# Turning the a2 terms of the attention layer on VectorE before they are stored to DRAM, and storing them from ScalarE's queue

## The chip, the cores and the metric

The kernel runs on one core of one Trainium2 chip. The metric is device time in microseconds (us) of one execution of the program; shown are the median of several executions and, beside it, one execution that was profiled. The engines are TensorE (PE, with its weight loads as PEld), VectorE (DVE), ScalarE (ACT), GpSimd (POOL) and SyncE (SP). SP, ACT and POOL also issue DMA transfers, each from its own queue; SPq, ACTq and POOLq in the profile are those queues.

## The reference, cut to what matters

Two layers work on N = 4096 nodes with C = 512 features, float32, with a dense 4096 x 4096 adjacency `adj`. Layer 0 averages the first 64 neighbours of each node, applies two linear maps with leaky ReLU, adds the input and normalizes the rows. Layer 1 is graph attention over its result `x`:

```python
Wh    = h @ W + bW
Wha1  = Wh @ a1 + b1          # one number per node
Wha2  = Wh @ a2 + b2          # one number per node: "the a2 terms"
e     = Wha1[:, None] + Wha2[None, :]
e     = where(e > 0, e, 0.2 * e)
e     = where(adj > 0, e, -9e15)
h_new = softmax(e, axis=1) @ Wh
x     = layernorm(x + h_new)
```

The change concerns only how the 4096 numbers of `Wha2`, computed with a node per partition, are laid out as a row that every partition can read.

## The kernel before, in words

Nodes are kept in 32 blocks of 128. Blocks 2t and 2t+1 hold the even and odd rows of the same 256 nodes, so node number = 256 t + 2 p + r for partition p and r = 0 or 1. The order of instructions on each engine is written out by hand; a tile framework only adds the waits. Each transfer that SP or ACT issues takes one of eight completion semaphores, which the program reuses in turn: an issue waits until the earlier transfer on the same semaphore has landed. SP and ACT share these eight. POOL's transfers have eight of their own.

Layer 0 runs first. Its second half is 2048 large matmuls on PE (L750), 128 for each pair of blocks of the adjacency, and `finish(i, g)` closes one block at a time: it makes the new row block, stores it to DRAM as `x1_d` (L719, POOL), and forms the products with the folded attention vectors, which leave Wha2 and Wha1 of block i in columns 0 and 1 of `e12` (`e12` is 128 partitions x 4 x 32 blocks; L724).

Layer 1 begins with a transition, and this is where the change lies. In DVE's order: the end of `finish` for block 31; small operations of 128x32 on the counts (L1132 to L1135); the addition of the biases to `e12` columns 0 and 1 (L1138, two instructions). In ACT's order: one logarithm of 128x32 into `e12` column 2 (L1136). Then POOL issues four kinds of transfer:

- `e12` column 0, stored to `e2_d` in DRAM (L1139, shown as `e_d<-e`): 16 KB. `e2_d` is indexed [t, p, r], so a partition p contributes, for each t, the two numbers r = 0 and 1. Source and target have only these two numbers, 8 bytes, in a run.
- `e12` columns 1 to 3, stored to `st_d` (L1142), 384 bytes a partition.
- `e2_d` read back as four quarters, each broadcast to 32 partitions, into `e2_n` (L1145, `e_n<-e_d`): 4 x 128 KB.
- `st_d` read back into `st_n` (L1147): 4 x 48 KB.

Meanwhile PE computes Wh = x W in steps j = 0 to 31 of 128 rows. Each step needs a turned block of x. `load_turned(j)` on SP (L807, shown as `w<-x_d`, as its tile is part of a tile named w) reads it in four transfers of 64 KB, in pieces of 512 bytes, into one of four slots (j mod 4); `turn_x1(j)` on DVE (L833) turns it in 32x32 squares into its operand form and frees the slot. Steps 0 to 3 are plain (matmuls L1185, ACT copies the result out of PSUM at L1189). The later steps, in pairs g = 2 to 15, use a scheme with seven products (`seven_wh`, matmuls L887). In it DVE forms sums of the turned blocks (L876, L877 at once, L882, L883 a step later), ACT copies a partial product (L906), and DVE adds it (L915, L911 for the first pair) into the PSUM bank into which PE then accumulates. `combine_wh` (L846 to L849) is DVE's work on finished pairs. The order on DVE around pair 3 is: `turn_x1(8)`, L882, L883, L846 to L849, `turn_x1(9)`, L876, L877, L915.

ACT issues the first loads of the adjacency codes, `load_nat` (L940, `nat<-code_d`, eight transfers of 64 KB), four after the first two copies L1189 and four after the third. Their first use is `cover` (L952, ACT), followed by `mask` on DVE (L962), which reads `e2_n`, and `score` (L945), which reads `st_n`. These weights of the attention fill a tile called `early`, until then scratch space; its quarter 3 is unused in its first 512 columns.

After step 31 PE runs the attention products (L1067) without a pause to the end.

Of the kernel before, what the change touches and what calls it, by code (L numbers as in the profile page):

```python
# [21 lines left out]
SQ = 32  # L22
# [10 lines left out]
def two_layer_adj_gnn(  # L33
# [16 lines left out]
    nc = tc.nc  # L50
# [3 lines left out]
    NT = NB // 2  # L54
# [35 lines left out]
    e12 = const.tile([P, 4, NB], F32, name="e12")  # L90
# [3 lines left out]
    e2_d = dram.tile([NT, P, 2], F32, name="e2_d")  # L94
# [42 lines left out]
    with ExitStack() as l0:  # L137
# [145 lines left out]
        with ExitStack() as la:  # L283
# [47 lines left out]
            def early(name):  # L331
                dt = I32 if name == "a" else BF16
                t = adj_p.tile([P, CH], dt, name=name).bitcast(F32)
                return t.rearrange("p (c q) -> p c q", q=C)

            raw = {}
            for name in ("nb", "line"):
                t = early("a")
                raw[name] = [t[:, c, :] for c in range(NC)]
            raw["w"] = []  # L340
            for k in range(2):
                t = early("left")
                raw["w"] += [t[:, c, :] for c in range(NC // 2)]
            early_rows = []
            for k in range(2):
                t = early("edge")
# [252 lines left out]
            for g in range(1, EDGE // 2):  # L599
                steps = idle  # L600
                q = done[0]
# [129 lines left out]
        for s in range(NB * NS):  # L731
            i, g = divmod(s, NS)
# [46 lines left out]
    early = wp.tile([P, NI, NS * SQ], F32, name="w")  # L779
# [356 lines left out]
    nc.scalar.activation(e12[:, 2, :], cnt, AF.Ln)  # L1136
    for k in range(2):
        nc.vector.tensor_scalar_add(e12[:, 1 - k, :], e12[:, 1 - k, :], ca[:, k : k + 1])  # L1138
    nc.gpsimd.dma_start(  # L1139
        e2_d.rearrange("t p r -> p t r"), e12[:, 0, :].rearrange("p (t r) -> p t r", r=2)  # L1140
    )
    nc.gpsimd.dma_start(st_d, e12[:, 1:4, :])  # L1142
    for n in range(4):
        quarter = e2_d.rearrange("(n t) p r -> n (t p r)", n=4)[n]
# [104 lines left out]
    p, rz = banks[NT - 1], rzs[NT - 1]  # L1249
# [62 lines left out]
```

## Time and profile before

| | us |
|---|---|
| median of 3 executions | 1566.76 (1563.01 to 1566.88) |
| the profiled execution | 1566.57 |
| its span | 1564.8 |
| PE busy in the span | 1549.1 (99%) |
| DVE, ACT, POOL busy | 1261.9, 980.1, 268.7 |
| first L1185 matmul, first L887 matmul, first L1067 matmul, from the span's start | 678.42, 692.15, 785.01 |

The span is the time from the first to the last instruction that the profiler recorded; 1.77 us of the execution lie outside it. Every time below that is a point in the execution counts from the span's start. In a row of the profile "out<-in" names the tiles written and read, and "[4.89 <-DVE acc L915]" says how long the engine idled before it and what ended that idleness. A row of the stretch view gives, for a stretch of time, the busy time of each engine with its number of instructions, then the clock that TensorE was granted as a share of its full one (PEclk), the mean busy share of the 16 DMA engines, and the bytes that they moved per second.

### The profile page before, as it was taken

How to read it: one execution, taken by the hardware profiler on the slowest of the kernel's cores; microseconds unless marked ns; L12 is line 12 of the kernel's file. 1: busy time of each engine (PE TensorE's matmuls, PEld its weight loads, DVE VectorE, ACT ScalarE, POOL GpSimd, SP SyncE). 2: the span in 40 equal slices, each digit the busy share in tenths (PEclk: the TensorE clock that was granted, in tenths of full speed). 3: DMA queues.
4: the chain of work that ended last, by engine and by line, in shares of the span. 5: the costliest groups of instructions: out<-in, count | busy, mean ns of one | idle time of the engine just before them, and what ended most of it. 6: DMA issues, size and time to landing. Idle time of an engine off the chain costs nothing.

```text
span 1564.8 us, 19133 instructions
## 1 busy us (share of the span) xinstructions
PE 1549.1 (99%) x6587; PEld 1244.3 (80%) x6587; DVE 1261.9 (81%) x2337; ACT 980.1 (63%) x1183; POOL 268.7 (17%) x425
## 2 busy tenths in 40 slices
PE   9999999999999999999999999999999999999998
PEld 5444468888888888868888888888888888888887
DVE  6888658999999998458888888787878878888765
ACT  2676558888888878426784675555765557755530
POOL 4454212222222122120001001110011100111101
PEclk9999999999999999999999999999999999999999
DMA  8866468999898787653222122221222212222102
GB/s 235 204 218 202 156 181 252 256 237 273 243 260 254 231 241 221 140 120 103 63 55 53 36 61 69 54 68 24 59 69 54 68 35 48 68 56 66 44 11 54
DMA packets 175345, 201.17 MB, mean 129 GB/s; under 512 B 101920, under 2 KB 135488, under 8 KB 167056
## 3 DMA queue, kind: packets, MB, share of 16 engines
q1 hardware_dynamic: 147472, 130.33, 29.8%
q0 software_dynamic: 26272, 67.66, 16.9%
q10 hardware_dynamic: 1504, 1.97, 0.5%
q8 instruction: 51, 0.84, 0.2%
q14 instruction: 46, 0.38, 0.1%
HBM read 141.03 MB, written 42.08 MB: 117 GB/s over the span
## 4 chain that ended last, share of the span: by engine, by line
PE 95%; DMA 2%; DVE 1%; issue 1%; ACT 0%; SPq 0%; POOLq 0%; ACTq 0%; DVEq 0%
PE acc L1067 35%; PE acc L750 30%; PE pt L1067 14%; PE acc L498 7%; PE acc L887 5%; PE acc L372 3%; DMA a<-in_adj_dram 1%; DMA nat<-code_d 1%; PE acc L1185 0%; PE pt L372 0%; PE pt L153 0%; DMA w<-x_d 0%; DVE edge L389 0%; DMA xb<-in_x_dram 0%; ACT edge L175 0%
## 5 line engine op out<-in xcount | busy, mean ns | idle before, releaser
L1067 PE MATMUL acc<-bt,s 128*128 128x256 f32 x1504 | 335.7, 379 | 0.0
L750 PE MATMUL acc<-y_hi,kt 128*128 128x512 f32 x824 | 320.5, 389 | 0.0
L750 PE MATMUL acc<-y_lo,kt 128*128 128x512 f32 x824 | 320.5, 389 | 0.0
L1067 PEld LDWEIGHTS acc<-bt,s 128*128 128x128 f32 x1504 | 285.8, 190 | 38.9
L952 ACT ACTIVATE w<-nat,few 128x1024 f32<-128x1024 uint8 x128 | 137.0, 1137 | 237.7 <-DVE a L1027 237.7
L1067 PE MATMUL acc<-bt,a 128*128 128x256 f32 x1056 | 239.0, 379 | 0.0
L1067 PE MATMUL pt<-bt,a 128*128 128x256 f32 x992 | 224.5, 379 | 0.0
L1067 PEld LDWEIGHTS acc<-bt,a 128*128 128x128 f32 x1056 | 200.6, 190 | 27.3
L1067 PEld LDWEIGHTS pt<-bt,a 128*128 128x128 f32 x992 | 188.5, 190 | 25.6
L277 ACT ACTIVATE kt<-ktb,few 128x1024 fp32r<-128x1024 uint8 x124 | 142.8, 1151 | 96.8 <-PE acc L750 79.6
L1027 DVE STREAM_TRANSPOSE a<-w 128x1024 f32<-128x1024 f32 x128 | 153.1, 1226 | 61.8 <-ACT w L1008 51.0
L126 POOL TENSOR_TENSOR rs<-ve,few 128x1 f32<-128x1 f32 x64 | 46.5, 726 | 809.7 <-DVE ve L124 797.1
L750 PEld LDWEIGHTS acc<-y_lo,kt 128*128 128x128 f32 x824 | 154.7, 188 | 32.2
L750 PEld LDWEIGHTS acc<-y_hi,kt 128*128 128x128 f32 x824 | 154.6, 188 | 32.1
L945 ACT ACTIVATE w<-w,st_n 128x1024 f32<-128x1024 f32 x128 | 149.3, 1233 | 16.1 <-DVE m L962 16.1
L1008 ACT ACTIVATE w<-w,nm 128x1024 f32<-128x1024 f32 x128 | 145.5, 1138 | 11.1 <-DVE nm L999 11.1
L962 DVE CUSTOM_DVE_ANT_0 w<-e_n,w 128x1024 f32<-128x1024 f32 x128 | 149.5, 1222 | 1.3
L175 ACT ACTIVATE edge<-a,few 128x2048 bf16<-128x2048 int32 x64 | 136.2, 2128 | 8.6 <-DMA a<-in_adj_dram 4.5
L223 ACT CAST code<-left 128x2048 uint8<-128x2048 bf16 x64 | 121.1, 1893 | 0.0
L206 DVE TENSOR_TENSOR left<-edge,left 128x2048 bf16<-128x2048 bf16 x64 | 78.4, 1225 | 2.2
L298 POOL DMA_DIRECT2D c<-in_x_dram x120 | 65.8, 555 | 69.7 <-DVE xt L325 54.3
L194 DVE TENSOR_TENSOR_SCAN left<-few,ends,left 128x1024 bf16<-128x1024 f32 x32 | 75.2, 2352 | 1.1
(225 smaller groups left out, 2009.6 us busy)
## 6 DMA issues: line engine op xcount, KB each, us to landing
a<-in_adj_dram SPq DMA_DIRECT2D x64, 1024.0 KB, 6.1
code_d<-code POOLq DMA_DIRECT2D x64, 256.0 KB, 4.3
nat<-code_d SPq DMA_DIRECT2D x248, 64.0 KB, 2.2
w<-x_d SPq DMA_DIRECT2D x128, 64.0 KB, 2.2
own<-in_x_dram SPq DMA_DIRECT2D x31, 256.0 KB, 3.2
own<-own_d POOLq DMA_DIRECT2D x31, 256.0 KB, 5.0
x_d<-own POOLq DMA_DIRECT2D x31, 256.0 KB, 5.0
c<-in_x_dram POOLq DMA_DIRECT2D x120, 64.0 KB, 5.0
```

Of the source, the lines that this page charges most:

```text
L175: nc.scalar.activation(edge_of[s], loaded.pop(s).rearrange("p (t q) -> p q t", q=2), AF.Sigmoid, bias=steep[:, 0:1], scale=STEEP, accum_ou ...
L206: nc.vector.tensor_tensor(left, e, left, ALU.mult)
L223: nc.scalar.copy(code.bitcast(U8).rearrange("p (t q) -> p q t", q=2), seen_of.pop(s))
L277: nc.scalar.activation(kts[s], bytes_.rearrange("p t (i r) -> p t r i", r=2), AF.Sigmoid, bias=steep[:, 1:2], scale=STEEP,)
L498: nc.tensor.matmul(bank, lhs[:, k, :], rhs[:, k, :], start=start and k == 0, stop=k == 1, skip_group_check=True,)
L750: nc.tensor.matmul(accs[i], kt[:, k // 2, k % 2, :], term[j], start=(j == 0 and term is y_hi), stop=(j == NB - 1 and term is y_lo),)
L945: nc.scalar.activation(dst, src, AF.Prelu, bias=bias, scale=scale, alpha=0.2)
L952: nc.scalar.activation(wts[b][:, i, :], nats[b, i // 2].bitcast(U8)[:, i % 2, :], AF.Relu, bias=far, scale=-FAR,)
L962: nc.vector.tensor_tensor_reduce(w_i, e2_n, w_i, 1.0, -3e38, ALU.subtract, ALU.max, m4s[b][:, i : i + 1])
L1008: nc.scalar.activation(w_i, w_i, AF.Exp, bias=nms[b][:, i : i + 1], accum_out=z4s[g][:, r, i : i + 1])
L1027: nc.vector.transpose(a[:, r].rearrange("p s (i a) -> p i s a", a=SQ), wts[2 * g + r][:, :, ts(k, 8 * SQ)].rearrange("p i (s x) -> p i s x ...
L1067: nc.tensor.matmul(banks[g][n], lhs[:, j, :], bt[:, 4 * k + j, rhs, :], start=(k == 0 and j == 0 and n == mate[0]), stop=(k == NP - 1 and ...
```

## The change

The a2 terms are turned in DVE's 32x32 squares before they are stored. Two transposes (r = 0 and 1), each of 128x32, write into 64 unused columns of the tile `early`. In each group of 32 partitions the 32 columns read are the 16 values of t of column 0 of `e12` and, as a filler, the 16 of column 1. After them partition 32 q + t holds the numbers of nodes 256 t + 64 q up to 64 q + 63 in a run of 64 numbers, 256 bytes. Four transfers (one for each q), each of 16 partitions, store them. They are issued from ACT's queue, after the logarithm L1136 and ahead of the first copy L1189 (L1194 in the changed file), whereas the store before was issued by POOL. Contents and layout of `e2_d` are the same. Lines below the change move down by five.

```diff
-    nc.gpsimd.dma_start(
-        e2_d.rearrange("t p r -> p t r"), e12[:, 0, :].rearrange("p (t r) -> p t r", r=2)
-    )
+
+    e2_t = early[:, 3, : 2 * SQ]
+    for r in range(2):
+        nc.vector.transpose(e2_t[:, r::2], e12[:, 0:2, r::2])
+    for q in range(4):
+        nc.scalar.dma_start(
+            e2_d.rearrange("t (q i) r -> q t (i r)", q=4)[q], e2_t[SQ * q : SQ * q + NT, :]
+        )
     nc.gpsimd.dma_start(st_d, e12[:, 1:4, :])
```

## The prediction

> **What bounds the kernel now.** I read the page first, then the chain of waits around the transition, then stretches of time, then DMA issues. The page says that PE is nearly always busy and carries the chain:
>
> ```profile
> PE   9999999999999999999999999999999999999998
> ...
> PE 95%; DMA 2%; DVE 1%; issue 1%; ACT 0%; SPq 0%; POOLq 0%; ACTq 0%; DVEq 0%
> ```
>
> So little is to be had: only time in which PE stands still or runs slowly. The chain, asked for from 670 to 800 us, shows the one place where the middle of the kernel leaves PE:
>
> ```profile
> 685.86 0.04 issue
> 685.90 0.44 ACTq L940
> ...
> 686.86 9.66 DMA nat<-code_d x2
> ...
> 697.41 1.26 SPq L807
> 698.67 0.05 issue
> 698.72 4.55 DMA w<-x_d
> ...
> 703.74 0.72 DVE a L833
> ...
> 705.29 0.43 DVE acc L915
> 705.72 0.04 issue
> 705.76 79.41 PE acc L887 x356
> ```
>
> Read backwards: PE resumed at 705.76 when L915 ended, L915 stood behind turn_x1(9), this waited for load_turned(9), and its issue waited for a nat transfer. The order of instructions in the timeline gives the idleness, and the stretch view gives the clock and the DMA:
>
> ```profile
> 705.76 2.07 PE L887 MATMUL acc<-s,bt 128*128 128x256 f32 x4 [4.49 <-DVE acc L915]
> ```
>
> ```profile
> 688.00:690.00 2.00, 2.00 (x6) 0.81 (x5) 1.86 (x3) 0.59 (x1) 0.39 (x1) 1.00 0.99 146
> 690.00:692.00 2.00, 2.00 (x6) 0.95 (x5) 1.33 (x3) 0.00 (x0) 0.00 (x0) 1.00 0.88 53
> 692.00:694.00 2.00, 2.00 (x9) 1.33 (x7) 0.88 (x3) 0.59 (x1) 0.00 (x0) 1.00 0.85 29
> ...
> 702.00:704.00 2.00, 0.00 (x0) 0.00 (x0) 0.26 (x1) 0.00 (x0) 0.00 (x0) 0.82 1.17 213
> 704.00:706.00 2.00, 0.24 (x1) 0.24 (x2) 1.93 (x5) 0.00 (x0) 0.00 (x0) 0.50 0.59 130
> 706.00:708.00 2.00, 2.00 (x5) 1.61 (x6) 1.90 (x6) 0.13 (x1) 0.00 (x0) 0.50 0.52 136
> 708.00:712.00 4.00, 4.00 (x15) 3.32 (x14) 2.15 (x5) 1.64 (x3) 0.00 (x0) 0.74 0.43 121
> ```
>
> Two things stand there. PE stops from 701.27 to 705.76, and its clock is halved from about 703.3 to 710.1 (0.82 of the first stretch, 0.74 of the last). And from 690 to 694 the DMA engines are 85% busy while moving 29 to 53 GB/s, against 146 and 213 around it. What is in flight then is e_d<-e, issued at 686.66 and landed 9.1 us later, and everything beside it is slow: from 690 to 694 the issues answer
>
> ```profile
> nat<-code_d ACTq DMA_DIRECT2D x2, 64.0 KB, 7.6
> w<-x_d SPq DMA_DIRECT2D x1, 64.0 KB, 7.1
> ```
>
> where the page's medians for these transfers from SP's queue are 2.2 us. I conclude that the 4096 pieces of 8 bytes clog the DMA engines until 695, and that the nat transfer issued at 688.92 therefore lands at 696.5; load_turned(9) uses its semaphore next, so it is issued from 696.58, not 691, and lands at 703.3.
>
> **What the Trainium skill says.** "DMA: Bandwidth & Descriptors", Specifications, asks for 512 bytes or more per piece and says that smaller ones are read, modified and written; its Rules for kernel authors say that a strided last dimension gives a descriptor per element. The trace fits the slowness (29 GB/s) but shows no read of the target. The same page, Issuing engines are not separate DMA queues, says that transfers of all queues share the 16 engines: nat (ACT) and w (SP) slowed by a POOL store agree. "TensorE: Matmul & The Clock Gate", What's actually happening, has the clock halve after about 3.4 us idle and return after as long busy: the trace has a stop of 4.49 us, and half clock for some 6.8 us.
>
> **The change, part by part.**
>
> *Removed: the clog.* L915 for pair 3 then no longer waits for a load. What is late next is DVE itself: it was ready for turn_x1(8) at 696.44 but started at 698.34 (idle 1.90, released by DMA w<-x_d). From that start to the end of L849 took 698.34 to 701.41, 3.07 us; from the start of turn_x1(9) to the end of L915, 703.74 to 705.71, 1.97 us. So 696.44 + 3.07 + 0.1 + 1.97 = 701.58, and PE resumes at 701.62, after an idleness of 0.35. Gain on the stop: 705.76 - 701.62 = 4.14 us.
>
> *Removed: the half clock.* 20 matmuls ran from 705.76 to 712.31, 6.55 us; at full clock a matmul of L887 starts every 0.216 us (28 in 6.04 us from 714.04), so 4.32. Gain 2.23. A stop of 0.9 us at 694.04 shows no drop, so none is expected after 0.35.
>
> *Does the load come in time?* turn_x1(9) is due at 699.6. load_turned(7) goes out once turn_x1(3) is done, at 686.6, and SP's issues follow each other 0.43 to 0.48 us apart in the trace. In the changed program every issue of loads 8 and 9 reuses the semaphore of an issue about four places ahead, so SP has four transfers of 64 KB under way, and a load of four takes about as long as one transfer takes to land. With 2.2 us each, load 8 goes out from 689.3 and load 9 from 691.9 to 693.7, landing by 696; with 3.5 us each, from 692.9 to 695.0, landing by 698.5. But e_n and st_n (0.7 MB) now run from about 690, not from 697, beside them; in their company loads took 4.1 to 5.2 us before. Both were then queued at once; here the start is spread. I take 3.5 and keep 5 as the bad end.
>
> *Added: two transposes on DVE.* Not in the trace at this size. From below, a 128x32 operation takes 0.18; from above, the 128x512 transpose L833 0.71. I take 0.2 each, 0.4 in all; nothing excludes 1.4, and in an in-order queue a gain is excluded. Behind them are turn_x1(3) to (5). PE wants turn_x1(3) for step 3 at 688.7 and has it at 686.5 instead of 686.05. DVE then idles 0.74 before L1196 and 1.57 before L911, both for PE or ACT following PE, so 0.4 is absorbed: 0.
>
> *Added: four issues on ACT's queue.* L940 issues show 0.43 to 0.48 apart: 4 x 0.45 = 1.8 us, from 685.95 (after the transposes) to 687.7. Behind them: copies L1189 0 and 1 move from 685.5 to some 687.9 and 688.4, the first four nat from 685.5-687.3 to 688-689.8, copy 2 from 688.9 to about 689.8, the other nat to 690.3-692.2, copy 3 to 692.4 against 692.35. ACT idled 2.37 and 2.85 us before copies 2 and 3, which is the cover. PE wants the bank of copy 2 at 692.15, and L906 at 694.07 follows copy 3, so copy 3 (0.59 us) may start at 693.4. I take 0; with transfers at 3.5 us the semaphore reuse moves copy 3 to about 694.2 and costs 0.7. A gain from this is excluded. The nat data is wanted at 708.14, over 10 us later.
>
> *The landing of the stores.* Nearest rows: z_d<-z, 4 KB, 1.4 us; x_d<-w, 256 KB, 2.3 us. I take 1.4 to 2.3. SP's load 7 reuses semaphores of the second and third store: its third issue moves from 687.45 to 688.4 at most, in the schedule above already.
>
> *Moved off POOL.* Its issue of 1.18 us goes; st_d may go at once; e_n waits for four ACT stores, from about 689.5 and not 696.27. First use of e_n is L962 at 712.39, so this gains nothing itself.
>
> **Sum.** 4.14 + 2.23 = 6.4 us gained, 0 to 0.7 lost: 6.2. After 706 PE waits nowhere for more than 0.3 us, and shifting PE, DVE and ACT together keeps that: from pair 6 on the L915s wait for PE again (idle 0.86, 1.77). Pair 5 is the narrow one: L915 comes 6.74 + 4.6 us after that of pair 3, its use two periods of 6.04 later, slack some 0.4. So profiled time 1566.57 - 6.2 = 1560.4, and against the median, 0.2 above that execution, 1560.5.
>
> **Rivals.**
>
> *A. The transfers collide instead* (22%). e_n, st_n, nat and loads 7 to 9 all run from 688 to 697. At 5 us each, load 9 is issued from 694.4 and lands at 701, L915 ends at 703 and PE stops 1.8 us: 2.7 gained, with the clock 4.9. For it: DMA share over 1 from 698 to 704. Against it: by packet times these transfers fill only some 6 of 10 us. Time 1561.9 to 1564.1.
>
> *B. Slower: ACT's queue is held* (6%). The pieces are still under 512 bytes. If the first store took 9.1 us as e_d did, the nat transfer that reuses its semaphore, and with it copies 2 and 3 and L906, wait: nat at 695, copy 3 at 699.5, L906 at 700.3 against 694.07. PE loses 6.2 where it lost nothing, with half clock 2.2, while the old 6.7 is only partly there: +2, 1569. It decides from a landing of 3.3 us on, when copy 3 passes 693.4. Against it: 64 pieces where 4096 were, and z_d<-z lands in 1.4.
>
> *C. The clog is not the pieces* (6%): the change doesn't do what it says, the slow transfers are congestion by count. Then time stays at 1566 to 1567. Against it: in no other stretch between 684 and 720 do the engines move so little at such a share (at 1.17 they move 213 GB/s).
>
> **Numbers.** The main case has 66%, at 1559.5 to 1561.5 before noise. A measurement of this kernel can tell about 0.3%, 4.7 us, from no change; the executions before spread 3.9 us. Main case and the upper part of A are faster: 0.73; the rest of A, C and a share of noise 0.22; B 0.05. The range takes the main case with the spread down, and A and most of C up: 1557 to 1565.5.
>
> **What would show it.** Right: no stretch of low GB/s at 85% share after 688; w and nat landing under 4 us; PE idle under 1 us between 694 and 712; PEclk 1.00 throughout; first L1067 matmul near 778.8, not 785.0; two 128x32 transposes of some 0.2. Wrong: a new stop of PE at 692 behind L1194 or L906 (B), load 9 landing after 699.6 (A), e_d landing over 3.3 us.

## The result, and the profile after

| | before | after |
|---|---|---|
| median of 8 executions, us | 1566.24 (1563.01 to 1566.88) | 1560.98 (1560.69 to 1564.03) |
| profiled execution, its span, us | 1566.57, 1564.8 | 1561.81, 1559.9 |
| PE busy in the span, us | 1549.1 | 1546.9 |
| first L1067 matmul, us from the span's start | 785.01 | 778.81 |

The ratio after/before is 0.9973, with a 95% interval of 0.9962 to 0.9984, which is 4.2 us of 1566. The medians lie 5.3 apart because six of the eight executions before took 1566.2 to 1566.9 and two 1563.0 and 1563.7, and the median lies in the upper group. The forecast was 1560.5.

On the page, PE's busy slices are what they were, and so, within one per cent, are the shares of the chain. A change of a third of a per cent is not seen there:

```profile
PE   9999999999999999999999999999999999999998
...
PE 95%; DMA 2%; DVE 2%; issue 1%; ACT 0%; ACTq 0%; POOL 0%; POOLq 0%; DVEq 0%
```

It is seen in the chain of waits from 670 to 800 us (columns: start, us, what). The link "nat transfer of 9.66 us, then a late load" is gone. The nat transfer takes 2.00. But the chain still runs through the loads of turned blocks, 8 and then 9, before it comes back to PE at 701.71, not 705.76:

```profile
685.49 0.35 ACTq L1144
...
687.63 2.00 DMA nat<-code_d
689.63 0.03 issue
689.65 5.25 DMA w<-x_d
694.92 4.64 DMA w<-x_d
...
699.68 0.72 DVE a L833
...
701.23 0.43 DVE acc L915
701.66 0.04 issue
701.71 77.27 PE acc L887 x356
```

In the timeline, PE's stop ahead of L915 fell from 4.49 to 0.76, and DVE shows why 0.76 is left: `turn_x1(9)` waited 0.59 for its load.

```profile
701.71 1.13 PE L887 MATMUL acc<-s,bt 128*128 128x256 f32 x4 [0.76 <-DVE acc L915]
```

```profile
699.68 0.71 DVE L833 STREAM_TRANSPOSE a<-w 128x512 f32<-128x512 f32 x1 [0.59 <-DMA w<-x_d]
```

The stretches (PE, PEld, DVE, ACT, POOL, then PEclk, DMA share and GB/s) show the two effects that the forecast named. From 690 to 694 the DMA engines, about as busy as before, now move 187 to 252 GB/s and not 29 to 53. From 702 on the clock is 1.00:

```profile
690.00:692.00 2.00, 2.00 (x6) 0.94 (x5) 1.66 (x4) 0.03 (x1) 2.00 (x5) 1.00 0.96 187
692.00:694.00 2.00, 1.71 (x8) 1.15 (x7) 0.55 (x2) 0.84 (x2) 1.62 (x3) 1.00 0.81 252
...
702.00:704.00 2.00, 2.00 (x11) 1.74 (x11) 1.90 (x6) 1.13 (x2) 0.00 (x0) 1.00 0.54 134
704.00:706.00 2.00, 2.00 (x11) 1.77 (x10) 1.93 (x5) 0.67 (x2) 0.00 (x0) 1.00 0.53 137
```

Of the DMA issues, the store (`e_d<-w`) and `st_d`, issued from 684 to 690, land in 1.7 and 1.8 us. Before, they took 9.1 and 8.4 (first the kernel before, issues from 683 to 689.5, then the changed kernel):

```profile
st_d<-e POOLq DMA_DIRECT2D x1, 48.0 KB, 8.4
e_d<-e POOLq DMA_DIRECT2D x1, 16.0 KB, 9.1
```

```profile
e_d<-w ACTq DMA_DIRECT2D x4, 4.0 KB, 1.7
st_d<-e POOLq DMA_DIRECT2D x1, 48.0 KB, 1.8
```

But those issued from 690 to 694 still take over 5 us, in company now of `e_n` and `st_n`, which have moved up to 689.4 and later:

```profile
nat<-code_d ACTq DMA_DIRECT2D x4, 64.0 KB, 5.3
w<-x_d SPq DMA_DIRECT2D x4, 64.0 KB, 5.5
```

One slip in the forecast: the store before had 2048 pieces of 8 bytes (16 KB), not 4096. No step of its sum used the number.

### The profile page after: what moved, and what is told of

Same layout as the page of the kernel before. It is cut to its first block, busy times and chain, and to the rows that moved or that the text cites. A ratio compares the mean times of both kernels' runs of the same rounds, so it can differ in the third digit from the quotient of the medians.

```text
span 1559.9 us, 19141 instructions
## 1 busy us (share of the span) xinstructions
PE 1546.9 (99%) x6587; PEld 1242.7 (80%) x6587; DVE 1261.9 (81%) x2339; ACT 980.1 (63%) x1183; POOL 266.4 (17%) x424
## 4 chain that ended last, share of the span: by engine, by line
PE 95%; DMA 2%; DVE 2%; issue 1%; ACT 0%; ACTq 0%; POOL 0%; POOLq 0%; DVEq 0%
PE acc L1067 35%; PE acc L750 30%; PE pt L1067 14%; PE acc L498 7%; PE acc L887 5%; PE acc L372 3%; DMA a<-in_adj_dram 1%; DMA w<-x_d 1%; PE pt L372 0%; PE pt L153 0%; PE acc L357 0%; DVE edge L389 0%; ACT edge L175 0%; DMA nat<-code_d 0%; DVE y_lo L421 0%
## 5 line engine op out<-in xcount | busy, mean ns | idle before, releaser
L1067 PE MATMUL acc<-bt,s 128*128 128x256 f32 x1504 | 335.7, 379 | 0.0
L1067 PEld LDWEIGHTS acc<-bt,s 128*128 128x128 f32 x1504 | 285.8, 190 | 38.9
L1067 PE MATMUL acc<-bt,a 128*128 128x256 f32 x1056 | 239.0, 379 | 0.0
L1067 PE MATMUL pt<-bt,a 128*128 128x256 f32 x992 | 224.5, 379 | 0.0
L1067 PEld LDWEIGHTS acc<-bt,a 128*128 128x128 f32 x1056 | 200.6, 190 | 27.3
L1067 PEld LDWEIGHTS pt<-bt,a 128*128 128x128 f32 x992 | 188.5, 190 | 25.6
```

The costliest lines, as they stand in the source:

```text
L1067: nc.tensor.matmul(banks[g][n], lhs[:, j, :], bt[:, 4 * k + j, rhs, :], start=(k == 0 and j == 0 and n == mate[0]), stop=(k == NP - 1 and ...
```

## The experiments

Two theories of why the time fell. **P**: the 8-byte pieces clog the DMA engines for everybody, and their going is the gain. **Q**: the gain comes from the move to ACT's queue, or from what moved with it. Ratios are to the kernel before, measured in the same session. Medians of the kernel before ranged from 1563.5 to 1566.2 between sessions, so ratios are compared, not medians.

### The changed kernel again, and its stores back on POOL's queue

The first is the changed kernel once more, for a ratio in the same session. The second differs from it in one thing:

```diff
-        nc.scalar.dma_start(
+        nc.gpsimd.dma_start(
             e2_d.rearrange("t (q i) r -> q t (i r)", q=4)[q], e2_t[SQ * q : SQ * q + NT, :]
```

> The changed kernel once more, beside the others on the same chip. Both theories: 5 to 6 us under the kernel before, PE stop ahead of L915 of pair 3 under 1 us, no half clock between 690 and 1550.

> The turned a2 terms (pieces of 256 bytes), but their four stores issued by POOL. Theory P (the 2048 pieces of 8 bytes clog the DMA engines): no stretch of low GB/s, loads land in under 5.5 us, within 1.5 us of the changed kernel, so 4 to 6 us under the kernel before. Theory Q (it is the queue: the store generated in software on POOL, or its late issue, is what costs): no gain, within 1.5 us of the kernel before, PE stop near 4.5 us.

Measured: 0.9974 [0.9964, 0.9984] for the changed kernel, 4.2 us between the medians and not the 5 to 6 expected, and 0.9971 [0.9960, 0.9981] with POOL's queue. On POOL the stretches move 207 to 247 GB/s, and PE does not stop at L915 at all:

```profile
688.00:690.00 2.00, 2.00 (x6) 0.89 (x5) 1.53 (x4) 0.00 (x0) 1.19 (x3) 1.00 0.72 207
690.00:692.00 2.00, 2.00 (x10) 1.39 (x8) 1.03 (x3) 0.58 (x1) 2.00 (x5) 1.00 1.02 237
```

The queue is worth nothing that these runs resolve (about 1.5 us); the new layout alone gives the gain.

### The 8-byte store on ACT's queue

The kernel before, with its store issued by ACT. This is the other half of the change:

```diff
-    nc.gpsimd.dma_start(
+    nc.scalar.dma_start(
         e2_d.rearrange("t p r -> p t r"), e12[:, 0, :].rearrange("p (t r) -> p t r", r=2)
```

> The kernel before, with its one store of 8-byte pieces issued by ACT where the changed kernel issues its four; no transposes. Theory P: the clog comes 1 us earlier and stays some 6 us long, transfers in it land in 7 us or more, PE stops for 3 us or more and the clock halves; time within 2 us of the kernel before, or slower, if ACT's queue is held behind it. Theory Q: 4 to 6 us under the kernel before.

Measured: 1.0007 [0.9999, 1.0015], no gain. The store lands in 7.9 us, and the clog is there, earlier, from 684:

```profile
686.00:688.00 2.00, 2.00 (x6) 0.95 (x5) 1.59 (x3) 0.59 (x1) 0.00 (x0) 1.00 0.59 19
688.00:690.00 2.00, 2.00 (x6) 0.87 (x5) 1.60 (x4) 0.00 (x0) 0.00 (x0) 1.00 0.74 36
```

PE now stops twice (the profiled execution is the slowest of thirteen, 2.7 us over their median):

```profile
695.38 1.13 PE L887 MATMUL acc<-s,bt 128*128 128x256 f32 x4 [3.61 <-DVE acc L911]
704.71 2.07 PE L887 MATMUL acc<-s,bt 128*128 128x256 f32 x4 [3.02 <-DVE acc L915]
```

The first stop is rival B's mechanism: ACT's nat issues wait for slow transfers, the copy and L906 stand behind them, and DVE's L911 waits 4.2 us for L906. Rival B's mechanism is thus a real danger of a slow store on ACT's queue; in the changed kernel the stores land in 1.7 us and it does not arise. Of the two halves of the change the layout carries the gain, and Q falls.

### The half clock by itself

The kernel before with its clog, but PE fed with ten matmuls of no use ahead of the one that waits for L915 (one spare PSUM bank, nothing reads it):

```diff
+            if g == PLAIN + 1:
+                idle = ps_s.tile([P, 2, HC], F32, name="pt")
+                for _ in range(10):
+                    nc.tensor.matmul(
+                        idle[:, 0], w11[:, 0, :P], w11[:, 0, :], start=True, stop=True,
+                        skip_group_check=True,
+                    )
             if new:
                 product_wh(xv[:, 0], sum_x(g, 2), t2)
```

> The kernel before, with ten matmuls of 128x256 (20 records, 4.3 us at full clock) of no use put on PE where it stops ahead of L915 of pair 3, into an idle PSUM bank. The clog and the wait stay. If the stop costs a half clock of 2.23 us beside its own 4.49, the clock stays at 1.00, PE resumes at the same 705.8, and the time is 1.8 to 2.4 us under the kernel before. If the half clock costs nothing (what follows is bound by DVE or ACT anyway), the time stays within 0.7 us of the kernel before.

Measured: 0.9988 [0.9982, 0.9995], which is 1.9 us of some 1564 (0.8 to 2.8). The clog stays, the useless work fills the stop, and the clock does not drop:

```profile
690.00:692.00 2.00, 2.00 (x9) 1.33 (x7) 0.91 (x3) 0.58 (x1) 0.00 (x0) 1.00 0.56 25
...
704.00:706.00 2.00, 2.00 (x11) 1.77 (x10) 1.93 (x6) 1.42 (x2) 0.00 (x0) 1.00 0.51 146
```

So some 2 us of the gain are the half clock, as the forecast's step of 2.23 had it, and the rest is the stop.

### Pieces of 32 bytes

The changed kernel, whose transposes leave gaps, so that the four stores have 512 pieces of 32 bytes, not 64 of 256:

```diff
-    e2_t = early[:, 3, : 2 * SQ]
+    e2_t = early[:, 3, : 4 * SQ].rearrange("p (a z) -> p a z", z=16)
...
-        nc.vector.transpose(e2_t[:, r::2], e12[:, 0:2, r::2])
+        nc.vector.transpose(e2_t[:, :, r:8:2], e12[:, 0:2, r::2])
...
-            e2_d.rearrange("t (q i) r -> q t (i r)", q=4)[q], e2_t[SQ * q : SQ * q + NT, :]
+            e2_d.rearrange("t (q a b) r -> q t a (b r)", q=4, b=4)[q],
+            e2_t[SQ * q : SQ * q + NT, :, :8],
```

> The changed kernel, with the turned terms laid out with gaps, so that each of the four stores has pieces of 32 bytes (512 pieces in all; 64 of 256 bytes in the changed kernel, 2048 of 8 before). If the cost goes with the number of pieces at the 3.1 ns that 2048 took (6.4 us from 688.7 to 695), the engines are slow for some 1.6 us, the stores land in 3 to 4 us, and the time is 0 to 2 us over the changed kernel. If any piece well under 512 bytes costs alike, it is as slow as 256 bytes, which means no cost: within 0.5 us of the changed kernel. If 8 and 32 bytes are both bad beyond count, the PE stop is over 3 us and the time near the kernel before.

Measured: 0.9974 [0.9965, 0.9982], the stores land in 1.7 us, and there is no clog:

```profile
686.00:688.00 2.00, 2.00 (x6) 0.85 (x5) 1.65 (x3) 1.07 (x2) 0.71 (x2) 1.00 0.69 175
```

The full 256 bytes are not needed. The pieces are larger here and also fewer, a quarter of 2048; no run has 2048 pieces of 32 bytes, so size and number are not parted. Nor does it follow that a piece of 32 bytes is free: 128 pieces for each store, with stores 0.43 us apart, could cost some 3 ns each and not be seen.

### The stores on SP's queue

The changed kernel with `nc.sync.dma_start` for the four stores, ahead of `load_turned(7)`.

> The turned terms stored by SP, ahead of load_turned(7), instead of by ACT. ACT's copies go back to their old place, and SP's loads 7 to 9 go out 1.8 us later. If load 9 is what DVE and then PE wait for (it landed 0.6 us late in the changed kernel), PE stops 2 to 2.5 us instead of 0.76 and the time is 1.2 to 2 us over the changed kernel, more if the clock halves. If SP has slack there, the time is that of the changed kernel within 0.5 us.

Measured: 0.9980 [0.9973, 0.9987]. PE stops 0.52 at L915 and DVE waits 0.4 for the load. The expected delay did not come. SP waited 3.8 us for the transposes with the store at the head of its queue, and in the changed kernel it waits 4.0 us at this place anyway, for DVE's `turn_x1`. Its loads land in 2.4 us there; those issued from 690 to 694 take 4.5. The intervals of ACT, POOL and SP overlap, so no queue is shown to be better than another.

### The term loads later

Left in the changed kernel was a stop of 0.76 (0.31 in its second profile). Rival A put such a rest down to `e_n` and `st_n` beside the loads. Here these eight loads go out after step 5 (a DVE memset on their target holds them back), from 696.6 on:

```diff
-    for n in range(4):
-        quarter = e2_d.rearrange("(n t) p r -> n (t p r)", n=4)[n]
...
+    def load_terms():
+        nc.vector.memset(e2_n[:, 0:1], 0.0)
+        for n in range(4):
+            quarter = e2_d.rearrange("(n t) p r -> n (t p r)", n=4)[n]
...
             seven_wh(g, h, lambda: weights_step(j))
+            if j == 5:
+                load_terms()
```

> The changed kernel, with the loads of e_n and st_n held back by a write of one column of e2_n on DVE after the sums of turned block 8, so that they run from some 698 and not from 690, away from loads 8 and 9. If they are what made loads 8 and 9 slow (5.5 us to landing in the changed kernel), these land in under 4 us, the wait of 0.59 before turn_x1(9) goes, and PE stops 0.3 to 0.45 us and not 0.76; the time falls by 0.3 to 0.5, too little to be told. If the eight nat transfers and the loads crowd each other, the landings stay near 5 us. A wait of DVE for e_n at the first mask would show that they were held too long.

Measured: the loads from 690 to 694 land in 2.3 us, where they took 5.5, and PE no longer stops at L915.

```profile
w<-x_d SPq DMA_DIRECT2D x8, 64.0 KB, 2.3
nat<-code_d ACTq DMA_DIRECT2D x1, 64.0 KB, 2.4
```

So the collision is real, and it is what made load 9 late. But the ratio is 0.9974 [0.9966, 0.9983], the same as without this edit: what it could win, 0.3 to 0.8 us, is below what these runs resolve.

### The clog put back, in three layouts and in half

If P holds, the old store added to the changed kernel as a spare, with nothing depending on it, must bring the old time back. Four kernels do this. POOL issues the spare store ahead of `st_d`; `e_d` keeps its new form:

```diff
+    spare_d = dram.tile([NT, P, 2], F32, name="spare_d")
...
+    nc.gpsimd.dma_start(
+        spare_d[:, :, 0:2].rearrange("t p r -> p t r"),
+        e12[:, 0, :].rearrange("p (t r) -> p t r", r=2),
+    )
     nc.gpsimd.dma_start(st_d, e12[:, 1:4, :])
```

> The changed kernel with one more store added, which is of no use: POOL writes column 0 of e12 a second time, to a spare tensor in DRAM with the layout of the kernel before ([t, p, r], 2048 pieces of 8 bytes, pieces of neighbouring partitions side by side). Nothing is left out. It is the suspected clog by itself, put back beside the new store. Theory P (the pieces of 8 bytes clog the DMA engines): the stretch 690 to 694 shows 20 to 60 GB/s at a share over 0.8; the spare store takes 8 to 9 us, w and nat land in 7 us or more there; PE stops 3 to 4.5 us at L915 with half clock after it; time 4 to 6.5 us above the changed kernel, so no less than 1563.5 and up to the kernel before's. Theory Q (the new store's queue or the earlier e_d is what gained): time within 1.5 us of the changed kernel.

> As f3_spare_old, but the spare tensor is [t, p, 64], so that each of the 2048 pieces of 8 bytes lies alone in 256 bytes of DRAM. The extra store is of no use; nothing is left out. If small pieces cost by their number and size, the clog is as in f3_spare_old: under 60 GB/s from 690 to 694, landings of 7 us or more, time 4 to 6.5 us above the changed kernel. If it is the sharing of neighbouring bytes in DRAM by pieces from several partitions that costs, the stretch stays over 150 GB/s and the time within 1.5 us of the changed kernel.

> The changed kernel with a useless extra store by POOL as in f3_spare_old (column 0 of e12, 2048 pieces of 8 bytes); nothing is left out. Only the spare tensor's layout differs: [p, t, 4], so that the 16 pieces of one partition lie 16 bytes apart within 256 bytes of DRAM, where in f3_spare_old neighbouring pieces come from different partitions and in f2_spare_apart each lies alone in 256 bytes. If nearness of successive pieces of one partition is what made f1_act_8_turned so slow: the spare store lands later than in f3_spare_old (7.7 us), at 10 us or more, and the time is 1 to 10 us above f3_spare_old's, 1567 to 1576. If f1_act_8_turned was slow for another reason (four transfers of 16 partitions, or ACT's queue): it lands in 6 to 8 us and the time lies between f2_spare_apart and f3_spare_old, 1563 to 1567.

> As f3_spare_old, but only for t = 0 to 7: 1024 pieces of 8 bytes, half as many; nothing is left out. If the clog grows with the number of pieces: the spare store lands in 4 to 5.5 us instead of 7.7, and the time is 0 to 2.5 us above the changed kernel, 1560 to 1563. If it has a fixed cost: landing over 6.5 us and time within 1.5 us of f3_spare_old's.

| spare store of 8-byte pieces | pieces | lands, us | ratio to before | above the changed kernel's 0.9974, us |
|---|---|---|---|---|
| `f2_spare_apart`: each alone in 256 bytes | 2048 | 6.0 | 0.9989 [0.9982, 0.9995] | 2.3 |
| `f3_spare_old`: beside those of neighbouring partitions | 2048 | 7.7 | 1.0005 [0.9996, 1.0014] | 4.9 |
| `g1_spare_own_line`: beside those of the same partition | 2048 | 10.5 | 1.0027 [1.0020, 1.0035] | 8.3 |
| `g2_spare_half`: as `f3_spare_old` | 1024 | 5.4 | 1.0000 [0.9991, 1.0009] | 4.1 |

(The last column is the difference of the ratios times 1565; each ratio is uncertain by 0.0006 to 0.001, 1 to 1.5 us, so 2.3 is a small step and 8.3 a clear one. The changed kernel was not run in these sessions; its ratio was 0.9973 and 0.9974 in two others.) The profiles give the same order more sharply. From the first matmul of layer 1 to the first L1067, one execution each, it is 106.59 us in the kernel before and 100.73 and 100.27 in the changed kernel; in the order of the table it is 103.63, 106.19, 109.33 and 104.82, so 3.1, 5.7, 8.8 and 4.3 above the mean of the two.

The issues of `f3_spare_old` from 684 to 690 show that one small store slows every queue's transfers:

```profile
w<-x_d SPq DMA_DIRECT2D x6, 64.0 KB, 7.3
e_n<-e_d POOLq DMA_DIRECT2D x3, 128.0 KB, 8.9
nat<-code_d ACTq DMA_DIRECT2D x4, 64.0 KB, 8.5
e_d<-w ACTq DMA_DIRECT2D x4, 4.0 KB, 1.6
st_d<-e POOLq DMA_DIRECT2D x1, 48.0 KB, 9.4
spare_d<-e POOLq DMA_DIRECT2D x1, 16.0 KB, 7.7
```

The new `e_d<-w`, just ahead of it, still lands in 1.6. So the new store was in place, and the clog alone ate the gain: with the old pieces back, the time is the kernel before's again. This settles P. Two details were not as expected. The low stretch came earlier, 84, 67 and 36 GB/s in the stretches from 686 to 692, and 106 from 692 to 694, where 20 to 60 was expected. And PE's stop was expected at L915 and came at L911 (5.89 us), by ACT's held queue, as in `e2_act_8`: ACT had nat issues to make in the time of the clog, and was held first.

The clog depends on number and on place. Half the pieces land 2.3 us sooner, which makes 2.2 ns for each of the 1024 left out. And 2048 pieces land later the closer in DRAM the successive pieces of one partition lie: 32 KB apart in `f2_spare_apart`, 1 KB in `f3_spare_old`, 16 bytes in `g1_spare_own_line`, with landings of 6.0, 7.7 and 10.5. Closeness of all pieces is not it: those of `f3_spare_old` fill 16 KB without a gap, those of `g1_spare_own_line` lie in 32 KB. From `f2_spare_apart` to `f3_spare_old` the neighbours from other partitions change too, so that step has two possible reasons. Of the two outcomes written down for `f2_spare_apart`, neither came; it lies between. The time of `g2_spare_half` lies above what was expected, and its interval overlaps that of `f3_spare_old`; the profiles, 104.82 against 106.19, have half the pieces cost 1.4 us less.

### The turned terms in 8-byte pieces

The changed kernel, with the transposes leaving gaps, so that ACT's four stores have 2048 pieces of 8 bytes, the 32 of one partition side by side:

```diff
-    e2_t = early[:, 3, : 2 * SQ]
+    e2_t = early[:, 3, : 4 * SQ].rearrange("p (i z) -> p i z", z=4)
...
-        nc.vector.transpose(e2_t[:, r::2], e12[:, 0:2, r::2])
+        nc.vector.transpose(e2_t[:, :, r], e12[:, 0:2, r::2])
```

> The changed kernel, whose turned terms are stored from ACT's queue in pieces of 8 bytes, 2048 of them (the transposes write into a layout with gaps, so that a run in SBUF is two numbers); the 32 pieces of one partition lie side by side in DRAM, 256 bytes in all. If small pieces cost by number and size: the stores take 6 to 9 us, the stretch 686 to 692 moves under 60 GB/s, ACT's nat issues are held as in e2_act_8 and PE stops 3 us or more at L911 or L915; time 1563 to 1566. If it is sharing of neighbouring bytes by several partitions: stores land under 3 us and the time is the changed kernel's, 1559 to 1561. Something between (stores of 3 to 4 us) would say that both count.

Measured: 1.0076 [1.0056, 1.0095], 16 us above the changed kernel, and outside every outcome that was written down. The chain goes through the store itself:

```profile
686.82 13.40 DMA e_d<-w
700.24 6.36 DMA w<-x_d
```

From 692 to 702 the engines move 2 to 30 GB/s. SP's loads wait 12.5 us for a store whose semaphore they reuse, and PE stops 3.87 and then 8.18 us. The next run, `g1_spare_own_line`, tested one difference: pieces of one partition near each other, everything else as in `f3_spare_old`. It went the same way, 10.5 against 7.7, so this nearness is part of it. But here it is 13.5 in the median; ACT's queue, four transfers of 16 partitions and a spacing of 8 bytes, not 16, were not separated from it.

## Why the prediction was right, point by point

**The clog** is removed: right, and its cause, the pieces, is shown by five runs (`e1_pool_256` and `e2_act_8` part the two halves of the change; `f3_spare_old` brings the time back; `f2_spare_apart` and `g1_spare_own_line` move it by layout). Rival C is out.

**The stop**, 4.14 forecast, measured 4.49 - 0.76 = 3.73. The mis-sized term is the landing of the loads: 3.5 was taken, with 5 as the bad end, and loads 8 and 9 took 5.25 and 4.64. One of the forecast's own signs of being right failed with it: w and nat were to land under 4 us, and those issued from 690 to 694 took 5.5 and 5.3. The profiled execution after reached L887 0.33 sooner than the one before, so the 699.6 at which the forecast had `turn_x1(9)` due is 699.27 on its clock. DVE was ready at 699.09 (699.68 less the idle 0.59), and load 9 landed at 699.56, 0.3 after it was due; had the load been there, the stop would have been some 0.2 (0.76 less 0.59), under the 0.35 forecast. This is rival A's collision, in small: `e6_terms_later` shows it. A's step that failed is load 9 landing at 701.

**The half clock**, 2.23 forecast, measured 79.41 - 77.27 = 2.14 in the chain, and 1.9 (0.8 to 2.8) by filling the stop.

**The two transposes**, 0.4 forecast, take 0.30 together (0.17 and 0.21 us each), and are covered as argued:

```profile
685.15 0.30 DVE L1142 STREAM_TRANSPOSE w<-e 128x32 f32<-128x32 f32 x2
```

**The issues on ACT** took 1.76 us (forecast 1.8), and the copies L1194 started where the schedule had them, less the same 0.33, the last at 692.08 (forecast 692.4), so PE lost nothing; it idled 0.93 at L911, as before:

```profile
685.49 1.76 ACTq L1144 DMA_DIRECT2D e_d<-w  x4
...
689.44 0.59 ACT L1194 COPY bt<-acc 128x512 f32<-128x512 f32 x1 [0.79 <-issue]
689.65 2.39 ACTq L940 DMA_DIRECT2D nat<-code_d  x4
692.08 0.59 ACT L1194 COPY bt<-acc 128x512 f32<-128x512 f32 x1 [2.05 <-PE acc L1190]
```

Rival B is out: the store landed in 1.7, under the 3.3 from which it decides.

**The sum.** L1067 was forecast near 778.8 and starts at 778.81, but by luck, by two errors that cancel: 5.87 gained at the transition for the 6.2 forecast, and a profiled execution that reached L887 0.33 sooner, which has nothing to do with the change.

**What the sum left out** is the end of the program. The last step of each chain, an issue of DVE's queue at the final output, came 6.2 us earlier (first the kernel before, then after):

```profile
1561.63 0.32 DVEq L1307
```

```profile
1555.44 0.33 DVEq L1312
```

But the span is only 4.9 shorter: from that step to the span's end it is 2.85 us before and 4.1 after. The last stores land 1.8 to 2.1 us after their issue in both; the rest is the closing of the program, where the profile shows nothing. So 5.9 gained at the transition, 0.3 by an earlier start and 1.3 given back make 4.9, between the 4.2 of the ratio and the 5.3 of the medians. The forecast took it that all after L1067 moves unchanged. Up to the last matmul that holds: from the first L1067 matmul to the last it is 773.33 us in every profile of every run. Why the tail is longer is open: it is 2.8 to 3.1 in the kernel before, `e4_fill_stop`, `f2_spare_apart`, `f3_spare_old` and `g1_spare_own_line`, and 4.1 to 4.2 in the changed kernel (both profiles), `e1_pool_256`, `e2_act_8`, `e3_act_32`, `e5_sp_256`, `e6_terms_later` and `f1_act_8_turned`. The first five have the same number of POOL transfers as the kernel before and the others have not; but `g2_spare_half` has it too, and its tail is 4.6. No run was made on it. It is worth 1 to 1.3 us, so a ratio between kernels of the two groups has that much in it which is not the transition.

## What to carry to other kernels

A store of 16 KB can be the costliest transfer of a kernel's stage: look for stretches where the GB/s fall while transfers are waiting, and at what all other transfers take there. The DMA share need not be high: it was 0.85 in the kernel before, but 0.27 to 0.40 in the clog of `g1_spare_own_line` from 690 to 696. Give such a store runs of 32 bytes or more (the smallest that was tried without harm), with a cheap transpose (0.30 us here) on an engine that has slack, before thinking about the queue that issues it. And price a stop of PE with the half clock that comes after it, here 2 us on top of 4.

## What the runs showed of the hardware that was not expected

**Small pieces can cost after they are sent.** In `e2_act_8` the trace's packets of the store, 2048 of 8 bytes at 7 ns each, all start between 684.2 and 685.6, yet the store lands 7.9 us after its issue and all other traffic crawls until 690. So in that run the time is not in the store's packets as the trace records them. It is not so in every layout: in `f1_act_8_turned`, on the same queue, the 2048 packets start from 686.8 to 694.0 and take 38 ns in the mean. The Trainium skill, "DMA: Bandwidth & Descriptors", Specifications, has pieces under 512 bytes read, modified and written. That landing times grow as successive pieces of a partition come closer in DRAM (6.0, 7.7, 10.5) would fit, but no run shows such a read; and 256 and 32 bytes, also under 512, cost nothing that could be seen.

**The half clock comes in units, on a fixed grid.** In the trace's clock records its length is 3.41 us after stops of 2.33 and 2.69 (`g2_spare_half`, `f2_spare_apart`), 6.83 after 3.02, 4.49 and 5.89 (`e2_act_8`, the kernel before, `f3_spare_old`) and 10.24 after 7.97 (`g1_spare_own_line`): one, two and three times 3.41. The full clock between lasts whole multiples of it too (696.3 us before the stop in the kernel before, 204 times 3.41; 1549.7 us in the changed kernel, 454 times). The Trainium skill, "TensorE: Matmul & The Clock Gate", What's actually happening, states a free-running window of 3413 ns, which agrees. Its threshold, a whole idle window, does not hold here. The clock records give the grid, and PE's busy time (its ends are modelled) gives the idleness in each window:

| run | window, us | clock in it | PE idle in it, us | clock after it |
|---|---|---|---|---|
| `e2_act_8` | 690.29 to 693.70 | full | 1.93 | full |
| `e2_act_8` | 693.70 to 697.12 | full | 1.68 | full |
| kernel before | 699.87 to 703.29 | full | 2.01 | half |
| `e2_act_8` | 700.53 to 703.94 | full | 2.25 | half |
| `e2_act_8` | 703.94 to 707.36 | half | 0.76 | half |
| `f2_spare_apart` | 694.37 to 697.78 | half | 0.32 | full |

In all fourteen profiles the clock was halved after every window with 2.01 us of idleness or more and after none with 1.93 or less; it came back after windows with at most 0.32, and not after those with 0.76 or more. So what counts is not how long the stop is but how much of it falls into one window. The 3.61 us at L911 in `e2_act_8` were split over two windows and cost nothing; the 2.33 in `g2_spare_half` fell into one. A stop of 2 to 4 us may cost the half clock or not, by where it falls; one of over 4.02 puts at least 2.01 into one window, wherever it falls.
